# Two banded layers: transposes by halves of rows, one PSUM bank per half, and a group norm moved ahead of the inverse roots

## The chip, the core and the metric

The kernel runs on one core of a Trainium2 chip. The metric is the device time of one execution in microseconds (us); lower is better. Five engines work side by side and are ordered only by semaphores: TensorE (PE in the profile, with its weight loads shown as PEld), VectorE (DVE), ScalarE (ACT), GpSimd (POOL) and SyncE (SP), which here issues the DMAs.

## The reference

Two layers of the same form act on an image x of 512 x 512 points with 64 channels, all in float32. Cut to one layer:

```python
g = group_norm(x)                      # 32 groups of 2 channels, over the whole image
xn = ln(g)                             # over the 64 channels
left  = (xn @ Wl + bl) * mask * sigmoid(xn @ Wlg + blg)
right = (xn @ Wr + br) * mask * sigmoid(xn @ Wrg + brg)
gate  = sigmoid(xn @ Wog + bog)        # 128 hidden channels each
out[i, j] = sum over k in i-4..i+4 of left[k, i] * right[k, j]    # per hidden channel
x = x + (ln(out) * gate) @ Wo + bo
```

## The kernel before

**Tiles.** The rows are cut into blocks of 64 with an overlap of 8 (`row_blocks`, L67), and the columns into chunks of 128. Partitions 0 to 63 hold the 64 rows of the block in the left half of the columns, partitions 64 to 127 the same rows in the right half. A `Unit` (L371) is 8 columns of that: a tile z of 128 partitions x 8 columns x 64 channels. A chunk has 16 units, and there are 18 chunks a layer.

**A unit's way.** `load` (L379) brings z by DMA. `affine` (L415) applies the group norm with two tensor operations on GpSimd (z<-z,ga and z<-z,gb). `inner_stats` (L420) takes the channel statistics on VectorE (sti<-z). `inner_norm` (L424) takes the mean off and multiplies by the inverse root on GpSimd (z<-z,sti and z<-z,rs). `transposed` (L430) turns z on TensorE, four transposes of 128x128 into one PSUM bank, and ScalarE copies them to the tile zT with 1.0 added, which also goes to DRAM for later. `right` (L459) projects zT in two calls of `projected` (L447), each into a pair of banks; ScalarE makes the sigmoid sg, and VectorE multiplies (RO<-banks,sg) into RO, the buffer of 128 hidden channels for a chunk. `left` (L469) does the same for the nine diagonals of the band, at the start of a layer only.

**Mixing and the way out.** `mix` (L511) makes the banded sum for 8 channels with 16 matmuls into a pair of banks; ScalarE and VectorE copy the halves back to RO. `out_stats` (L543) takes statistics of RO (sto<-RO). `norm` (L582) writes the normalized result into the tile on (one buffer), with eight ScalarE operations. `gates` (L594) projects the gate from the recalled zT (zg) into two banks, and ScalarE makes two tiles gate. `turned` (L613) transposes on with eight transposes of 128x128 into two banks, and VectorE adds ob and multiplies by the gate into ZH. `end` (L643) projects with Wo into one bank, VectorE adds the residual XR, and SyncE stores. `biased` (L637) adds the bias to XR on GpSimd. `sums` (L662), in layer one only, adds up the second layer's group statistics into acc.

**The inverse roots.** `solve` (L549) makes, once in four steps, the inverse roots for the inner and the outer norm: VectorE prepares the variances and a first guess rs, and GpSimd refines it in ten small operations and makes two more (`rsqrt`, L134).

**PSUM.** `one_bank` (L128) takes from a pool of three single banks in layer one and four in layer two; `two_banks` (L131) takes from two pairs that projections and mixes share.

**Order.** The function `layer` (L674) writes the order out by hand: for each step t it issues the parts, and every engine keeps that order, since the helper class InOrder (L354) records each operation. So nearly all lines of the profile carry one number, L362, the helper's, and one goes by the names of the tiles. In a step t the order is: loads and recalls; statistics of RO; affine of the units planned for t; gates of t; half of the inner statistics; projections of t; inner_norm for t+2; transposed for t+1; turned and biased for t; the rest of the statistics; end of t-1; sums of t-2; the solve, where t is 3 modulo 4; norm for t+1; the mixes planned for t. Of the 16 steps of a chunk (t modulo 16), steps 0 to 9 have mixes (2, 1, 2, 2, 1, 2, 1, 2, 2, 1) and steps 10 to 15 have none. Outputs begin 30 steps after the first unit, so a layer is 30 steps of input alone, 258 of both, and 30 of output alone. The statistics of RO fall once in a step, twice in steps 10 and 11, and not at all in 8 and 9. An affine falls once in a step, twice in steps 2 and 6, and not at all in 11 and 15.

Of the kernel before, what the change touches and what calls it, by code (L numbers as in the profile page):

```python
# [8 lines left out]
F32 = mybir.dt.float32  # L9
I32 = mybir.dt.int32  # L10
AF = mybir.ActivationFunctionType
ALU = mybir.AluOpType
# [4 lines left out]
P = 128  # L17
WIN = 4
NEAR = 2 * WIN + 1
S = 64  # L20
JC = 128
JW = 16
JU = 8
JQ = 4
NU = JC // JU
# [54 lines left out]
def tile_two_banded_layers(  # L80
# [8 lines left out]
    H = layers[0]["Wl"].shape[1]  # L89
    x, out = x[0], out[0]  # L90
# [22 lines left out]
    ident = const.tile([P, P], F32, name="ident")  # L113
# [239 lines left out]
    w = views(pack)  # L353
# [70 lines left out]
    def inner_norm(u: Unit):  # L424
        z = u.z.rearrange("p (k t) c -> p k t c", t=2)
        m = u.mean.unsqueeze(3).broadcast_to([P, JU // 2, 2, D])
        en.gpsimd.tensor_tensor(z, z, m, ALU.subtract)
        en.gpsimd.tensor_tensor(u.z, u.z, last(u.rs, D), ALU.mult)

    def transposed(u: Unit):  # L430

        u.t = ztp.tile([P, JU // 2, P], F32, tag="zT", name="zT")
        pt = one_bank()
        for k in range(JU // 2):
            en.tensor.transpose(
                pt[:, k * P : (k + 1) * P],
                u.z[:, 2 * k : 2 * k + 2, :].rearrange("p j c -> p (j c)"), ident,
            )
        en.scalar.activation(u.t.rearrange("c k p -> c (k p)"), pt, AF.Identity, bias=1.0)
        if u.near is None:  # L440
            en.sync.dma_start(later[u.at], u.t)

    def place(k: int, e: int) -> int:

        return k // 2 * 4 + 2 * e + k % 2
# [136 lines left out]
    def norm(o: Out):  # L582
        o.on = onp.tile([P, JU, H], F32, tag="on", name="on")
        for j in range(JU):
# [8 lines left out]

    def gates(o: Out, w: dict):  # L594
        b = o.blk
        o.g = []
        pgs = [
            one_bank()[:, : 2 * JQ * b.m].rearrange("h (k p) -> h k p", p=b.m) for e in range(2)
        ]
# [7 lines left out]
        for pg in pgs:  # L607
            g = gp.tile([H, 2 * JQ * (S - WIN)], F32, tag="gate", name="gate")
            g = g[:, : 2 * JQ * b.m].rearrange("h (k p) -> h k p", p=b.m)
            en.scalar.activation(g, pg, AF.Sigmoid)  # L610
            o.g.append(g)

    def turned(o: Out, w: dict):  # L613

        b = o.blk
        for e in range(2):
            pt = one_bank()
            for k in range(JQ):
                en.tensor.transpose(
                    pt[:, k * P : (k + 1) * P], o.on[:, place(k, e), :], ident  # L620
                )
            zh = ZH[(2 * o.n + e) % len(ZH)]
            en.vector.scalar_tensor_tensor(
                zh[:, :, : b.m], pt.rearrange("h (k p) -> h k p", p=S)[:, :, b.lo : b.hi], w["ob"], o.g[e],
                ALU.add, ALU.mult,
            )

    def rows_of(v: bass.AP, o: Out, e: int):
# [14 lines left out]
    def end(dst: bass.AP, o: Out, w: dict):  # L643
        m = o.blk.m
        po = one_bank().rearrange("i (j c) -> i j c", c=D)
        for k in range(JQ):
            for e in range(2):
                for n in range(2):

                    en.tensor.matmul(  # L650
                        po[n * S : (n + 1) * S, 2 * k + e, :],
                        lhsT=ZH[(2 * o.n + e) % len(ZH)][:, 2 * k + n, :], rhs=w["Wo"],
                        start=True, stop=True,
                    )
# [19 lines left out]
    def layer(src: bass.AP, dst: bass.AP, w: dict, stats: bool, then=None):  # L674
# [27 lines left out]
        for n in range(0, NEAR * JQ, JU):  # L702
            t = 3 + n // JU * 2
# [3 lines left out]
        def inputs(t: int) -> list:  # L707
            return [d[t] for d in (units, lefts) if t in d]
# [3 lines left out]
        loads, affines, inners = {}, {}, {}  # L712
# [14 lines left out]
        for u in early:  # L727
            load(src, u)
        yield
        A, sti, sto = {}, {}, None  # L730
        for t in range(min(loads), last_t + 3):
            if then and t == max(units) + 2:
                then()
# [10 lines left out]
            for o in looks.get(t, []):  # L744
                if sto is None:
                    sto = sm.tile([P, NB // 2, 6], F32, tag="sto", name="sto"), []
# [1 line left out]
                for k in range(JU // 2):  # L748
                    out_stats(o, st[:, len(os) * (JU // 2) :], k)
                os.append(o)  # L750
            for u in affines.get(t, []):
                affine(u, en.vector if u.at < NU + 4 else en.gpsimd)
            if t in outs:
                gates(outs[t], w)

            todo = []
            for at, u in inners.get(t, []):
# [4 lines left out]
                n = len(us) * (JU // 2)  # L762
# [10 lines left out]
                    left(lefts[t], q, w)  # L773
            for u in inputs(t + 2):
                inner_norm(u)
            for u in inputs(t + 1):
                transposed(u)
            if t in outs:
                turned(outs[t], w)
                biased(outs[t], w, stats)  # L780
            for v in todo[len(todo) // 2 :]:
                inner_stats(*v)
# [4 lines left out]
            if t % 4 == 3:  # L787
                st, us = sti.pop((t + 5) // 4, (None, []))
                so, os = sto or (None, [])
                sto = None  # L790
                if us or os:
                    solve(w, us, os, st, so)
            if t + 1 in outs:
                norm(outs[t + 1])
            for n, (c, h0) in enumerate(mixes.get(t, [])):
                mix(c, A[c, h0 // HA], h0, [True, n + 1 < len(mixes[t])])

# [128 lines left out]
```

## Time and profile before

| | |
|---|---|
| median of 3 runs | 5162.48 us (5158.28 to 5162.59) |
| profiled execution | 5160.82 us |
| its span, first to last instruction | 5158.9 us |
| granted TensorE clock, mean | 0.970 |
| chain that ended last: share on TensorE | 73% (POOL 9%, DVE 5%, DMA 5%) |
| transposes of z | 2344 of 128x128, 395.6 us busy |
| transposes of on | 4608 of 128x128, 632.3 us busy |
| ScalarE's norm (on) | 4608, 494 ns each |
| GpSimd waited for VectorE's rs | 512.8 us in 148 waits |

A line of the profile gives source line, engine, operation, the tile written <- the tiles read, and the shapes; in the view in order of time it begins with the start from the span's beginning and the length, and in brackets stands how long the engine had been idle and who released it. "64*128" in a TensorE line is the part of the array used, rows x columns. A float32 matmul shows as two records, a transpose as one. A record of TensorE lasts longer than the distance to the next, because matmuls are pipelined: the distance between starts is what a matmul takes away from the engine.

### The profile page before, as it was taken

Reading aid. Unit: us, or ns where it says so; the run is one execution under the profiler, and the core shown is the slowest. Engines: PE = TensorE matmul, PEld = TensorE weight load, DVE = VectorE, ACT = ScalarE, POOL = GpSimd, SP = SyncE. Lnnn points to the kernel's source line nnn. Section 1 sums busy time; section 2 is a strip of 40 time slices with the busy share of each in tenths; the row PEclk is TensorE's granted clock in tenths of the full one; section 3 lists DMA queues with packets and bytes.
Section 4 is the critical chain, followed back from the end, with each engine's and each line's share of the span. In section 5 each row is a group of like instructions: output and inputs, shape, how many; then the busy total and the mean of one; then the engine's idle time right before and its main releaser. Section 6 shows DMA issues by size and latency. Waiting matters only on the chain.

```text
span 5158.9 us, 159784 instructions
## 1 busy us (share of the span) xinstructions
PE 4536.4 (88%) x60138; PEld 3756.4 (73%) x60138; DVE 3656.7 (71%) x9445; ACT 3793.4 (74%) x8328; POOL 3821.0 (74%) x4739
## 2 busy tenths in 40 slices
PE   1037999999999999999995599999999999999999
PEld 0025788888888888888873378888888887888886
DVE  6864677777777777777766467777777777777776
ACT  0013788888888888888884268888888888888888
POOL 0037888888888888888733588888888888888863
PEclk9988999999999999999998799999999999999999
DMA  7924666666666666666663457667677776667766
GB/s 318 387 62 127 176 190 191 190 192 190 193 190 190 190 191 190 191 192 192 187 169 108 105 172 200 196 197 200 194 200 199 199 199 195 194 199 200 200 186 172
DMA packets 905291, 981.45 MB, mean 190 GB/s; under 512 B 114210, under 2 KB 641608, under 8 KB 900168
## 3 DMA queue, kind: packets, MB, share of 16 engines
q1 hardware_dynamic: 897248, 948.49, 63.6%
q10 hardware_dynamic: 7272, 22.73, 1.1%
q8 instruction: 477, 7.82, 0.7%
q14 instruction: 294, 2.41, 0.2%
HBM read 658.42 MB, written 312.46 MB: 188 GB/s over the span
## 4 chain that ended last, share of the span: by engine, by line
PE 73%; POOL 9%; DMA 5%; DVE 5%; ACT 3%; issue 2%; SPq 2%; another core or an unknown queue 0%; ACTq 0%; POOLq 0%; DVEq 0%
PE banks L362 37%; PE bank L362 34%; POOL z L362 5%; POOL rsqrt L362 2%; DMA left_of<-nothing 2%; ACT on L362 2%; PE acc L362 2%; SPq L362 2%; DVE RO L362 1%; DVE ZH L362 1%; DMA gn_x<-in_x_dram 1%; POOL rs L362 1%; DMA z<-mid_x 1%; ACT gate L362 1%; DVE sti L362 0%
## 5 line engine op out<-in xcount | busy, mean ns | idle before, releaser
L362 ACT ACTIVATE on<-RO,nm,rs 128x128 f32<-128x128 f32 x4608 | 1878.3, 494 | 183.9 <-PE bank L362 178.3
L362 PE MATMUL banks<-pack,zT 64*128 64x256 f32 x9360 | 1219.7, 389 | 133.9 <-ACT zT L362 79.3
L362 PEld LDWEIGHTS banks<-pack,zT 64*128 64x128 f32 x9360 | 974.4, 193 | 413.6 <-issue 172.7
L362 PE MATMUL banks<-RO,A 64*64 64x128 f32 x18432 | 1154.6, 277 | 0.0
L362 PEld LDWEIGHTS banks<-RO,A 64*64 64x64 f32 x18432 | 1082.4, 183 | 26.7 <-issue 3.3
L362 ACT ACTIVATE sg<-banks 128x512 f32<-128x512 f32 (+1 forms) x1188 | 684.0, 589 | 323.4 <-PE banks L362 207.0
L362 DVE TENSOR_TENSOR RO<-banks,sg 128x512 f32<-128x512 f32 x1152 | 748.8, 682 | 231.0 <-ACT sg L362 230.1
L362 DVE COPY RO<-banks 128x512 f32<-128x512 f32 x360 | 249.0, 692 | 930.6 <-ACT RO L362 930.6
L362 DVE SCALAR_TENSOR_TENSOR ZH<-bank,pack,gate 128x448 f32<-128x448 f32 (+1 forms) x1152 | 742.6, 684 | 99.2 <-PE bank L362 61.4
L362 DVE BATCH_NORM_STATS2 sto<-RO 128x6 f32<-128x256 f32 x2304 | 797.8, 412 | 1.2
L362 POOL TENSOR_TENSOR z<-z,gb 128x512 f32<-128x512 f32 x536 | 685.2, 1278 | 42.0
L362 POOL TENSOR_TENSOR z<-z,ga 128x512 f32<-128x512 f32 x536 | 685.8, 1280 | 0.1
L362 PE MATMUL bank<-zg,pack 64*128 64x448 f32 (+1 forms) x2304 | 665.5, 597 | 18.6 <-DVE ZH L362 16.3
L362 PE MATMUL bank<-pack,ZH 128*64 128x64 f32 x18432 | 677.9, 228 | 3.0 <-ACT zT L362 0.5
L362 PEld LDWEIGHTS bank<-pack,ZH 128*64 128x64 f32 x18432 | 597.9, 140 | 103.6 <-ACT zT L362 76.7
L362 ACT ACTIVATE gate<-bank 128x448 f32<-128x448 f32 (+1 forms) x1152 | 566.5, 542 | 128.8 <-PE bank L362 127.9
L362 POOL TENSOR_TENSOR z<-z,rs 128x512 f32<-128x512 f32 x586 | 617.7, 1054 | 46.0
L362 PE MATMUL bank<-ident,on 128*128 128x128 f32 x4608 | 632.3, 279 | 14.7 <-ACT gate L362 12.1
L362 POOL TENSOR_TENSOR z<-z,sti 128x512 f32<-128x512 f32 x586 | 623.4, 1064 | 0.0
L362 ACT COPY RO<-banks 128x512 f32<-128x512 f32 x792 | 440.1, 585 | 225.7 <-PE banks L362 224.6
L362 DVE BATCH_NORM_STATS2 sti<-z 128x6 f32<-128x128 f32 x2344 | 549.0, 283 | 66.6 <-POOL z L362 66.6
L362 PEld LDWEIGHTS bank<-ident,on 128*128 128x128 f32 x4608 | 532.9, 144 | 73.9 <-ACT on L362 24.2
(137 smaller groups left out, 3725.3 us busy)
## 6 DMA issues: line engine op xcount, KB each, us to landing
later<-zT SPq DMA_DIRECT2D x576, 256.0 KB
A<-left_of SPq DMA_DIRECT2D x576, 256.0 KB
zg<-later SPq DMA_DIRECT2D x576, 256.0 KB
z<-in_x_dram SPq DMA_DIRECT2D x576, 128.0 KB
z<-mid_x SPq DMA_DIRECT2D x576, 128.0 KB
gn_x<-in_x_dram SPq DMA_DIRECT2D x16, 4096.0 KB
XR<-in_x_dram SPq DMA_DIRECT2D x448, 112.0 KB
mid_x<-XR SPq DMA_DIRECT2D x448, 112.0 KB
```

The costliest lines, as they stand in the source:

```text
L362: return lambda *a, **k: tc.keep_in_program_order(f(*a, **k))
```

## The change

1. **Transposes by halves.** In `transposed` and `turned` each 128x128 transpose becomes two of 64 rows: partitions 0 to 63 and 64 to 127, each with its own 64x64 corner of the identity, in the 64*128 tiling that projections and gate use. The two halves write into different PSUM banks. So there are eight transposes with 64 moving columns for z, and 16 for on.
2. **Banks.** In steady state z goes into a pair of `two_banks`; lefts and the units up to number 16 use two single banks. The copy to zT is split off into `kept`; it reads both banks in one operation, or takes two operations for the single banks. on goes into two single banks by half of the rows rather than by columns, so ZH is now filled by halves, and `end` reads it accordingly. The gate becomes one tile of twice the size, with one buffer.
3. **Order within a step.** turned comes ahead of transposed, three of the eight norm operations for t+1 come between the transposes of z and their copy, and the other five stay where norm was.
4. **Group norm ahead of the roots.** In a step with a solve (t modulo 4 is 3, beyond the first chunk) the affine operations planned for t+1 are issued on GpSimd just ahead of the solve.

```diff
@@ def transposed
+        if u.near is None and u.at > NU:
+            u.pt = [two_banks().rearrange("c (n x) -> c n x", n=2)[:, :, : JU // 2 * S]]
+            halves = [u.pt[0][:, n] for n in range(2)]
+        else:
+            halves = [one_bank()[:, : JU // 2 * S] for n in range(2)]
+            u.pt = [h.unsqueeze(1) for h in halves]
+        for k in range(JU // 2):
+            for n in range(2):
+                part = slice(n * S, (n + 1) * S)
+                en.tensor.transpose(
+                    halves[n][:, k * S : (k + 1) * S],
+                    u.z[part, 2 * k : 2 * k + 2, :].rearrange("p j c -> p (j c)"),
+                    ident[part, part],
+                )
+
+    def kept(u: Unit):
         u.t = ztp.tile([P, JU // 2, P], F32, tag="zT", name="zT")
-        pt = one_bank()
-        for k in range(JU // 2):
-            en.tensor.transpose(
-                pt[:, k * P : (k + 1) * P],
-                u.z[:, 2 * k : 2 * k + 2, :].rearrange("p j c -> p (j c)"), ident,
-            )
-        en.scalar.activation(u.t.rearrange("c k p -> c (k p)"), pt, AF.Identity, bias=1.0)
+        to = u.t.rearrange("c k (n p) -> c n k p", n=2)
+        for n, pt in enumerate(u.pt):
+            en.scalar.activation(
+                to[:, n : n + pt.shape[1]], pt.rearrange("c n (k p) -> c n k p", p=S),
+                AF.Identity, bias=1.0,
+            )
@@ def gates
-            g = gp.tile([H, 2 * JQ * (S - WIN)], F32, tag="gate", name="gate")
+        g = gp.tile([H, 4 * JQ * (S - WIN)], F32, tag="gate", name="gate")
@@ def turned
+        pts = [one_bank().rearrange("h (x p) -> h x p", p=S) for n in range(2)]
         for e in range(2):
-            pt = one_bank()
             for k in range(JQ):
-                en.tensor.transpose(
-                    pt[:, k * P : (k + 1) * P], o.on[:, place(k, e), :], ident
-                )
-            zh = ZH[(2 * o.n + e) % len(ZH)]
+                for n, pt in enumerate(pts):
+                    part = slice(n * S, (n + 1) * S)
+                    en.tensor.transpose(
+                        pt[:, e * JQ + k, :], o.on[part, place(k, e), :], ident[part, part]
+                    )
+        for n, pt in enumerate(pts):
             en.vector.scalar_tensor_tensor(
-                zh[:, :, : b.m], pt.rearrange("h (k p) -> h k p", p=S)[:, :, b.lo : b.hi], w["ob"], o.g[e],
-                ALU.add, ALU.mult,
+                ZH[(2 * o.n + n) % len(ZH)][:, :, : b.m], pt[:, :, b.lo : b.hi], w["ob"],
+                o.g[:, n], ALU.add, ALU.mult,
             )
@@ def end
-                        lhsT=ZH[(2 * o.n + e) % len(ZH)][:, 2 * k + n, :], rhs=w["Wo"],
+                        lhsT=ZH[(2 * o.n + n) % len(ZH)][:, e * JQ + k, :], rhs=w["Wo"],
@@ def layer
-            for u in affines.get(t, []):
+            for u in affines.pop(t, []):
                 affine(u, en.vector if u.at < NU + 4 else en.gpsimd)
+            if t % 4 == 3 and t > NU:
+                then_affine = affines.pop(t + 1, [])
...
+            if t in outs:
+                turned(outs[t], w)
             for u in inputs(t + 1):
                 transposed(u)
+            if t + 1 in outs:
+                norm(outs[t + 1], 0, 3)
+            for u in inputs(t + 1):
+                kept(u)
             if t in outs:
-                turned(outs[t], w)
                 biased(outs[t], w, stats)
...
+                for u in then_affine:
+                    affine(u, en.gpsimd)
+                then_affine = []
                 if us or os:
                     solve(w, us, os, st, so)
             if t + 1 in outs:
-                norm(outs[t + 1])
+                norm(outs[t + 1], 3, JU)
@@ pools
-    gp = ctx.enter_context(tc.tile_pool(name="gp", bufs=2))
+    gp = ctx.enter_context(tc.tile_pool(name="gp", bufs=1))
```

More of the change, by code (lines that the diff above doesn't have):

```diff
@@ L580, in solve, with norm @@
                 o.rs, o.nm = ro[:, n * JU : (n + 1) * JU], nm[:, n * JU : (n + 1) * JU]
-    def norm(o: Out):
-        o.on = onp.tile([P, JU, H], F32, tag="on", name="on")
-        for j in range(JU):
+    def norm(o: Out, j0: int, j1: int):
+        if j0 == 0:
+            o.on = onp.tile([P, JU, H], F32, tag="on", name="on")
+        for j in range(j0, j1):
             en.scalar.activation(
@@ L595, in gates @@
         b = o.blk
[L596 to L599, printed above, removed]
+        n = 2 * JQ * b.m
+        pgs = [one_bank()[:, :n].rearrange("h (k p) -> h k p", p=b.m) for e in range(2)]
         for e, pg in enumerate(pgs):
@@ L606, in gates @@
             )
-        for pg in pgs:
-            g = gp.tile([H, 2 * JQ * (S - WIN)], F32, tag="gate", name="gate")
-            g = g[:, : 2 * JQ * b.m].rearrange("h (k p) -> h k p", p=b.m)
-            en.scalar.activation(g, pg, AF.Sigmoid)
-            o.g.append(g)
+        g = gp.tile([H, 4 * JQ * (S - WIN)], F32, tag="gate", name="gate")
+        for e, pg in enumerate(pgs):
+            en.scalar.activation(
+                g[:, e * n : (e + 1) * n].rearrange("h (k p) -> h k p", p=b.m), pg, AF.Sigmoid
+            )
+        o.g = g[:, : 2 * n].rearrange("h (x n p) -> h n x p", n=2, p=b.m)
     def turned(o: Out, w: dict):
         b = o.blk
+        pts = [one_bank().rearrange("h (x p) -> h x p", p=S) for n in range(2)]
         for e in range(2):
-            pt = one_bank()
             for k in range(JQ):
-                en.tensor.transpose(
-                    pt[:, k * P : (k + 1) * P], o.on[:, place(k, e), :], ident
-                )
-            zh = ZH[(2 * o.n + e) % len(ZH)]
+                for n, pt in enumerate(pts):
[4 more added lines that the diff above has]
+        for n, pt in enumerate(pts):
             en.vector.scalar_tensor_tensor(
-                zh[:, :, : b.m], pt.rearrange("h (k p) -> h k p", p=S)[:, :, b.lo : b.hi], w["ob"], o.g[e],
-                ALU.add, ALU.mult,
+                ZH[(2 * o.n + n) % len(ZH)][:, :, : b.m], pt[:, :, b.lo : b.hi], w["ob"],
+                o.g[:, n], ALU.add, ALU.mult,
             )
@@ L729, in layer @@
         yield
-        A, sti, sto = {}, {}, None
+        A, sti, sto, then_affine = {}, {}, None, []
         for t in range(min(loads), last_t + 3):
```

## The prediction

> **What bounds the kernel now.** I read the page's busy shares first, then one step on TensorE and the same step on VectorE in the order of time, then GpSimd in a step without mixing, then the totals of the waits. All times are from the one profiled execution (5160.82 us); start times of single records are quoted where a merged line hides them.
>
> ```profile
> PE 4536.4 (88%) x60138; PEld 3756.4 (73%) x60138; DVE 3656.7 (71%) x9445; ACT 3793.4 (74%) x8328; POOL 3821.0 (74%) x4739
> ```
>
> TensorE at 88% is 96% inside the layers (96.55 of 100 us in the stretch from 1500 to 1600). One step with one mix, TensorE, columns start, length, what:
>
> ```profile
> 1506.58 1.02 PE L362 MATMUL bank<-zg,pack 64*128 64x448 f32 x4
> 1507.44 1.89 PE L362 MATMUL banks<-pack,zT 64*128 64x256 f32 x16
> 1509.26 0.66 PE L362 MATMUL bank<-ident,z 128*128 128x128 f32 x4
> 1509.76 1.04 PE L362 MATMUL bank<-ident,on 128*128 128x128 f32 x8
> 1510.72 1.15 PE L362 MATMUL bank<-pack,ZH 128*64 128x64 f32 x32
> 1511.70 0.64 PE L362 MATMUL acc<-XR 120*64 120x65 f32 x16
> 1512.27 2.10 PE L362 MATMUL banks<-RO,A 64*64 64x128 f32 x32
> ```
>
> No line starts with a wait: this step is TensorE's work alone, 7.72 us to the next gate. I count from its gate: second projection issued by 2.58, transposes from 2.68 to 4.05, mix from 5.69. VectorE in the same step:
>
> ```profile
> 1507.32 0.69 DVE L362 COPY RO<-banks 128x512 f32<-128x512 f32 x1 [3.81 <-ACT RO L362]
> 1507.93 1.40 DVE L362 BATCH_NORM_STATS2 sto<-RO 128x6 f32<-128x256 f32 x4
> 1509.24 0.48 DVE L362 BATCH_NORM_STATS2 sti<-z 128x6 f32<-128x128 f32 x2
> 1509.63 1.28 DVE L362 TENSOR_TENSOR RO<-banks,sg 128x512 f32<-128x512 f32 x2
> ```
>
> This chain hangs on the end of the previous mix: copy, eight statistics, then the product of `right`. The first product ends at 1509.63+0.68 = 1510.31, 3.72 after the gate. Nobody needs it before the mix at 5.69 today: 1.9 us of slack. GpSimd, six steps later, and TensorE's answer:
>
> ```profile
> 1548.68 1.19 POOL L362 TENSOR_TENSOR XR<-XR,fewer 120x512 f32<-120x512 f32 x1 [2.04 <-PE bank L362]
> 1556.16 0.29 POOL L362 TENSOR_TENSOR rsqrt<-rs 128x64 f32<-128x64 f32 x1 [6.29 <-DVE rs L362]
> ```
>
> ```profile
> 1560.68 1.27 POOL L362 TENSOR_TENSOR z<-z,ga 128x512 f32<-128x512 f32 x1
> 1562.03 1.27 POOL L362 TENSOR_TENSOR z<-z,gb 128x512 f32<-128x512 f32 x1
> 1563.26 1.06 POOL L362 TENSOR_TENSOR z<-z,sti 128x512 f32<-128x512 f32 x1
> 1564.39 1.04 POOL L362 TENSOR_TENSOR z<-z,rs 128x512 f32<-128x512 f32 x1
> ```
>
> ```profile
> 1565.49 0.66 PE L362 MATMUL bank<-ident,z 128*128 128x128 f32 x4 [2.55 <-POOL z L362]
> ```
>
> GpSimd sits 6.29 us idle for VectorE's `rs`, then does the roots, then the group norm, and only then the z that TensorE waits for.
>
> **What the skill says.** "TensorEngine Tiling (Array Packing)", Key Properties: a change of tiling mode drains TensorE, and tiles work in parallel. The trace agrees: the eight projection pairs issue every 0.216 (the two of a pair 7 ns apart), so the next could start at 1509.17, but z starts at 1509.26 and its first transpose takes 0.165 instead of 0.109. A change costs 0.09 + 0.06 = 0.15 us. The same page, Gotcha 1, wants different row tiles in different PSUM banks, which is why each half gets a bank. "TensorE: Matmul & The Clock Gate", PE-mode transpose, gives about 275 ns for a bf16 transpose in a kernel; here the record lasts 279 to 293, but the next starts after 109, and 109 is what I use. "PSUM — Partial Sum Buffer", Engine vs sequencer instructions: VectorE, ScalarE and GpSimd are strict FIFO; the lines above show it, the group norm does not pass the waiting roots.
>
> **Part 1, transposes by halves.** Per step 12 transposes (4 of z, 8 of on) become 12 pairs with 64 moving columns each. No row shows a transpose in 64*128 tiles. Nearest: `bank<-pack,ZH`, 64 columns in pairs, 16 pairs from 1510.72 to 1511.70, less 0.05 for the first = 0.058 a pair. The weight side allows that: the second LDWEIGHTS of the 128x128 transposes starts 58 ns after the first. I take 0.058. Bounds: 0.054 (half of 109), and 0.116, if the halves of a pair follow each other or if the weights take as long as the gate's 64x128 ones (its first pair lasts 0.107 longer than its second). TensorE saves 12×(0.109−0.058) = 0.61, and the mode change behind the projection (0.15): 0.76 us a step, if nothing else comes in.
>
> **Part 2, where the halves go.** In the order of the changed program, z goes into `two_banks`, two buffers that projections and mixes share; its first transpose waits for a VectorE count that is the first product of `right`, and for GpSimd's z. Behind it on TensorE stand the output projection, the sums and the mix. So in a step behind a mix: on ends at 2.58+8×0.058 = 3.05; z starts at 3.72+0.055 (the hand-over from VectorE, as from ZH at 1547.48 to 1547.54) = 3.77, 0.72 stalled; it takes 0.056 for its first weights and 4×0.058, to 4.06; from the transposes' end to the mix is 1.64 as before: 5.70. Before: 5.69. **The saving is spent on a wait.** The steps of a chunk, by t mod 16: 1, 2, 4, 5, 6 have this product at 3.72: +0.01 each. In 3 and 7 two units' statistics put it at 4.12: +0.41 each. In 8 and 9 no statistics of RO stand ahead, 3.31: −0.40 each. Step 0: −0.08. Sum over the ten mixing steps: about 0. The later zT copy (behind three `on`) ends near 5.1, ahead of the second mix that needs its bank at 7.5: free. ScalarE's eight `on` end at 7.15, before the mix does: free.
>
> **Part 3, steps 10 to 15, without mix.** Steps 10 to 12 are VectorE's (6.2 of 6.4 us busy, eight RO statistics each in the first two). z stalls there up to 2.2 us, but TensorE's later results still arrive before VectorE's queue comes to them, so VectorE keeps its pace: layer one 18.85 instead of 19.05, layer two 18.5 instead of 18.1. At the solve of step 11 the group norm for step 12 (2×1.29 = 2.58) now runs inside the 6.29 idle; its z was loaded at 1540.7. So the z for step 13 is ready 2.58 sooner, and the 8.31, 9.88 or (layer two) 10.5 us of step 13 fall to ScalarE's pace: gates 0.88, sg 1.04, zT 0.52, on 8×0.394 = 3.15, 5.6 us, its 0.34 wait for the transposes being gone since on is transposed first and three `on` lie ahead of zT. Steps 14 and 15 go at the same 5.6; GpSimd needs 5.87 with a group norm in each, but starts 2.58 ahead: its z is ready 0.3 to 0.6 before it is wanted. Layer one: 18.85+3×5.62 = 35.7, against 39.1 and 40.4 in alternate chunks (1541.14 to 1580.24, 1668.60 to 1709.00): −4.05. Layer two: 35.2 against 39.06 (4235.44 to 4274.50): −3.9. With 15 such chunks a layer: 61+58 = 119 us. The other solves gain nothing; TensorE does not wait there.
>
> **Part 4, the ends.** Each layer's first 30 steps: z shorter by 0.2 in ten mixing steps (4 us for both layers), and the 5.31 and 4.12 us waits for POOL at 541.56 and 3031.16 shorter by 2.58 (5). Ten mixing steps per layer after the last unit have no z and no stall: 8×0.051+0.15 = 0.56 each (11). Twenty last steps of layer one go at 4.50 because `on` and its transposes alternate on one buffer; the transposes shrink by 0.45 there (9). Together 29. The gate tile (one buffer for two halves) costs nothing: ScalarE's gate comes after both ZH products today as well.
>
> **Sum.** 5160.8−119−29 = 5013 for the profiled execution; it lies 1.7 below the median of the runs shown, so 5014.
>
> **Rivals.** (a) Pairs at 0.116: z ends at 4.29, +0.23 in 310 mixing steps (71) and some 10 at the ends: 5095. The gate's weights speak for it, the transposes' 58 ns against. (b) No cost of the z wait, if VectorE's product comes sooner than I read: ten steps gain 0.6 to 0.76, 310×0.7 = 215 more: about 4800. TensorE's 96% speaks for it, the 3.72 against. (c) Slower: a half-transpose costs as much as a whole one and halves do not overlap, 0.218 a pair. on ends at 4.32, z at 5.25, +1.19 in 310 mixing steps, 370 us lost, and some 60 in steps 13 to 15, against 148 gained: about 5440. It decides from about 0.16 a pair (z must end by 4.06+0.48). The profile has no transpose in this tiling, so it can't be excluded; the projections' pairs, 7 ns apart, speak against it.
>
> **Chances.** Forecast 0.73, (a) 0.11, (b) 0.05, (c) and other losses 0.11. Unsure in the forecast itself: ScalarE's pace in steps 13 to 15 (at 5.9 instead of 5.6: +27), the hand-over (0.1 instead of 0.055: +14), pairs at 0.054 and a shorter chain (−30). With (a)'s end inside, 4975 to 5105; (b) and (c) are left out. Faster by over 0.2% (what a measurement of this kernel can tell from no change): 0.87; within: 0.03; slower: 0.10.
>
> **What would show it.** Single starts of the new transposes 58 ns apart per pair; TensorE idle ahead of `banks<-ident,z`, released by DVE RO, of 300 to 400 us in all (0.7 in most mixing steps, about 2 in step 10); steps 1 to 9 of a chunk unchanged in sum at 79 us in layer one, steps 13 to 15 at about 5.6 each; GpSimd's 512.8 us of waiting for `rs` (the waits' total) down by 150 to 200, half of it in step 11. I am wrong if the pairs lie further apart than 60 ns, if mixing steps shorten by over 0.2 on average, or if step 13 stays above 7.

## The result, and the profile after

| | before | after |
|---|---|---|
| median of the runs | 5161.35 us (5158.28 to 5162.59) | 5192.92 us (5190.45 to 5194.06) |
| ratio, 95% interval | | 1.0061 (1.0044 to 1.0079) |
| span of the profiled execution | 5158.9 us | 5191.7 us |
| granted TensorE clock, mean | 0.970 | 0.962 |

The change makes the kernel 0.6% slower; the forecast was 5014. The page's first part, for the kernel after:

```profile
PE 4206.4 (81%) x67090; PEld 3583.6 (69%) x67090; DVE 3720.7 (72%) x9445; ACT 3759.0 (72%) x8372; POOL 3825.2 (74%) x4739
```

TensorE works 330 us less than before (4536.4) and the span is 33 us longer: the transposes did get cheaper, and some 360 us of new idle time took the place of that. Where it lies can be seen when the steps of a chunk are laid beside each other. A step is the time from one gate (`bank<-zg,pack`) to the next; means over the 15 chunks of each layer that have all 16 steps:

| steps (t mod 16) | layer one, before | after | layer two, before | after | both layers, 15 chunks each |
|---|---|---|---|---|---|
| 0 | 9.63 | 12.40 | 9.48 | 13.08 | +96 us |
| 1 to 9, sum | 78.75 | 79.75 | 74.53 | 75.47 | +29 us |
| 10 to 12, sum | 19.06 | 19.65 | 18.10 | 18.82 | +20 us |
| 13 to 15, sum | 20.74 | 16.86 | 21.06 | 16.43 | -128 us |

With what lies around these chunks (+16 us) that makes the 33 us of the spans. Step 13 lost its stall, as forecast; **one step in sixteen, step 0, takes three quarters of that back** (96 of 128 us). One such step before, VectorE and then TensorE, in the order of time (start, length, what; in brackets how long idle before and released by whom):

```profile
1580.98 0.67 DVE L362 TENSOR_SCALAR var<-sti 128x32 f32<-128x32 f32 x1
...
1582.01 0.20 DVE L362 TENSOR_SCALAR rs<-var 128x64 int32<-128x64 int32 x1
```

```profile
1582.92 0.66 PE L362 MATMUL bank<-ident,z 128*128 128x128 f32 x4
...
1585.99 3.95 PE L362 MATMUL banks<-RO,A 64*64 64x128 f32 x64
```

TensorE in one such step after:

```profile
1717.41 1.02 PE L362 MATMUL bank<-zg,pack 64*128 64x448 f32 x4
...
1720.00 0.66 PE L362 MATMUL bank<-ident,on 64*128 64x64 f32 x16
1722.95 0.46 PE L362 MATMUL banks<-ident,z 64*128 64x64 f32 x8 [2.30 <-POOL rsqrt L362]
...
1724.33 1.09 PE L362 MATMUL acc<-XR 120*64 120x65 f32 x16
1725.35 4.96 PE L362 MATMUL banks<-RO,A 64*64 64x128 f32 x64
```

The transposes of z stand 2.30 us idle. The named releaser, GpSimd's `rsqrt`, is only the count that came last by the profile; what z needs is its pair of banks, and that is VectorE's first product of `right`. After the stall the same instructions take longer: the sums 1.09 where other steps have 0.64, the two mixes 4.96 instead of 3.94. VectorE, from the third of the solve's five operations on, and GpSimd:

```profile
1718.58 1.05 DVE L362 TENSOR_SCALAR var<-var 128x32 f32<-128x32 f32 x1
1719.54 0.17 DVE L362 TENSOR_SCALAR nm<-sto 128x32 f32<-128x32 f32 x1
1719.66 1.24 DVE L362 TENSOR_SCALAR rs<-var 128x64 int32<-128x64 int32 x1
1720.82 1.39 DVE L362 BATCH_NORM_STATS2 sto<-RO 128x6 f32<-128x256 f32 x4
1722.14 1.27 DVE L362 TENSOR_TENSOR RO<-banks,sg 128x512 f32<-128x512 f32 x2
```

```profile
1718.29 1.30 POOL L362 TENSOR_TENSOR XR<-XR,fewer 120x512 f32<-120x512 f32 x1
1719.55 1.30 POOL L362 TENSOR_TENSOR z<-z,ga 128x512 f32<-128x512 f32 x1
```

Two of the solve's small VectorE operations, `var<-var` on 32 columns and `rs<-var` on 64, last 1.05 and 1.24 us. The first starts 0.29 after GpSimd's `XR<-XR` does and ends at 1719.63, as that operation ends (1719.59); the second starts 0.11 after the moved group norm's first operation and ends at 1720.90, as that one does (1720.85). VectorE's statistics and the product come behind them in its order: the first product ends 5.4 us after the gate.

The Trainium skill has this in "SBUF — State Buffer", Who interferes with whom: VectorE and GpSimd share a pair of ports as a lock, an operation of VectorE in a 2-port mode (tensor_scalar can be one) or with two inputs in SBUF contends for it, and whoever comes second blocks for the other's whole instruction. The trace agrees, and shows which operations are spared. Medians (of the lengths) over all records of the kernel after, without and with a GpSimd operation beside them:

| VectorE operation | alone | beside GpSimd | records beside |
|---|---|---|---|
| rs<-var | 0.195 us | 1.233 us | 40 |
| var<-var | 0.181 us | 1.051 us | 32 |
| var<-sti | 0.170 us | 0.676 us | 46 |
| sti<-z (statistics) | 0.280 us | 0.281 us | 1876 |
| sto<-RO (statistics) | 0.409 us | 0.409 us | 2100 |
| RO<-banks,sg (reads PSUM) | 0.680 us | 0.681 us | 934 |
| var<-sto (two inputs in SBUF) | 0.188 us | 0.186 us | 36 |
| nm<-sto | 0.175 us | 0.169 us | 32 |
| z<-z,gb on VectorE, 128x512 (two inputs in SBUF) | 0.691 us | 1.411 us | 30 |

The last row comes from the start of the layers; the 16 of its 30 records that begin beside GpSimd's 128x512 `z<-z,rs` take 1.41 us, the others 0.69. So it is not only small operations that are held. `var<-sto` and `nm<-sto` are mostly spared in this kernel; in `nm<-sto` above, VectorE starts just as one GpSimd operation gives way to the next. In e2_group_norm_only below both are stretched too. Of the solve's five operations 97 records in the kernel after last over 0.4 us: each begins while a GpSimd operation runs and ends within 0.06 us of the end of one. The profile before already held 25 such records; the `var<-sti` of 0.67 us above is one, beside GpSimd's `XR<-XR`.

The span of the solve's five operations ahead of step 0 is 0.94 and 0.75 us before (layers one and two, means of 16 chunks) and 2.84 and 3.21 after; ahead of the other solves it stays at 0.72 to 0.85 after. Before, GpSimd mostly sat waiting for `rs` while VectorE made it. The change filled just that waiting time with the group norm.

The last part of the loss is TensorE's clock. The same stretch cut into windows (columns: window, length, busy time of PE, PEld, DVE, ACT, POOL with instructions, then the granted clock, the busy share of the DMA engines and GB/s):

```profile
1720.00:1723.00 3.00, 0.70 (x20) 0.59 (x17) 3.00 (x7) 2.06 (x5) 2.76 (x5) 1.00 0.71 208
1723.00:1724.30 1.30, 1.30 (x40) 1.23 (x42) 1.30 (x3) 0.85 (x2) 1.05 (x4) 1.00 0.79 267
1724.30:1727.71 3.41, 3.41 (x46) 3.29 (x42) 0.98 (x2) 1.68 (x5) 2.92 (x8) 0.50 0.77 223
1727.72:1731.00 3.28, 3.28 (x50) 2.89 (x48) 0.01 (x1) 1.66 (x3) 3.20 (x4) 1.00 0.24 76
```

Full clock until 1.35 us after the end of the stall, then half the clock for 3.41 us, then full again. What decides this is looked at under "The clock" below.

### The profile page after: what moved, and what is told of

Same layout as the page of the kernel before. It is cut to its first block, busy times and chain, and to the rows that moved or that the text cites. A ratio compares the mean times of both kernels' runs of the same rounds, so it can differ in the third digit from the quotient of the medians.

```text
span 5191.7 us, 173015 instructions
## 1 busy us (share of the span) xinstructions
PE 4206.4 (81%) x67090; PEld 3583.6 (69%) x67090; DVE 3720.7 (72%) x9445; ACT 3759.0 (72%) x8372; POOL 3825.2 (74%) x4739
## 5 line engine op out<-in xcount | busy, mean ns | idle before, releaser
L362 ACT ACTIVATE on<-RO,nm,rs 128x128 f32<-128x128 f32 x4608 | 1934.1, 498 | 12.3 <-PE bank L362 12.1
L362 PE MATMUL banks<-pack,zT 64*128 64x256 f32 x9360 | 1176.9, 391 | 104.3 <-ACT zT L362 54.5
L362 PEld LDWEIGHTS banks<-pack,zT 64*128 64x128 f32 x9360 | 939.5, 195 | 412.5 <-issue 195.4
L362 PE MATMUL banks<-RO,A 64*64 64x128 f32 x18432 | 1175.3, 280 | 14.3 <-ACT zT L362 14.3
L362 PEld LDWEIGHTS banks<-RO,A 64*64 64x64 f32 x18432 | 1103.4, 184 | 41.4 <-ACT zT L362 17.1
L362 PE MATMUL bank<-zg,pack 64*128 64x448 f32 (+1 forms) x2304 | 617.8, 606 | 2.5 <-DVE ZH L362 2.4
L362 PE MATMUL banks<-ident,z 64*128 64x64 f32 x4336 | 254.8, 234 | 443.0 <-DVE RO L362 267.6
L362 POOL TENSOR_TENSOR XR<-XR,pack 120x512 f32<-120x512 f32 (+1 forms) x352 | 418.7, 1190 | 198.2 <-DMA XR<-mid_x 87.7
```

Source lines behind the costliest of these rows:

```text
L362: return lambda *a, **k: tc.keep_in_program_order(f(*a, **k))
```

## Experiments

Three theories. **T:** in step 0 GpSimd's work blocks VectorE's solve; the product comes late; z waits for it because of its new bank; TensorE idles and gets a lower clock. **R1:** GpSimd is merely late, since the group norm stands ahead of the roots. **R2:** z's new bank alone makes step 0 slow, and the group norm is harmless. "Five" is the mean span of the solve's five VectorE operations ahead of step 0, layers one and two.

| kernel | median us | ratio to before (95%) | step 0, layers one, two | five |
|---|---|---|---|---|
| e1_group_norm_back | 5211.6 | 1.0093 (1.0077 to 1.0110) | 10.00, 11.11 | 1.52, 1.99 |
| e2_group_norm_only | 5070.4 | 0.9823 (0.9808 to 0.9838) | 9.93, 9.87 | 3.10, 2.71 |
| e3_not_at_15 | 5131.3 | 0.9939 (0.9924 to 0.9954) | 10.13, 11.03 | 1.57, 2.16 |
| e7_behind_first_root | 5131.7 | 0.9937 (0.9922 to 0.9952) | 10.14, 11.46 | 1.58, 2.12 |
| e8_bias_too | 5099.6 | 0.9878 (0.9863 to 0.9893) | 9.65, 9.70 | 0.72, 1.38 |
| e4_z_behind_sums | 4981.6 | 0.9650 (0.9636 to 0.9664) | 9.78, 11.61 | 2.61, 3.26 |
| e9_both | 4937.2 | 0.9564 (0.9549 to 0.9580) | 9.01, 8.76 | 0.72, 1.43 |
| e10_on_by_halves | 5216.2 | 1.0105 (1.0090 to 1.0120) | 10.25, 8.90 | 0.72, 1.95 |
| e12_group_norm_no_collision | 5073.1 | 0.9824 (0.9811 to 0.9838) | 9.67, 9.17 | 0.72, 0.72 |
| e13_all_but_11 | 4918.1 | 0.9528 (0.9515 to 0.9541) | 9.01, 8.76 | 0.72, 1.37 |

### The change without the group norm, and the group norm without the change

```diff
@@ layer, against the kernel after (e1_group_norm_back)
-            if t % 4 == 3 and t > NU:
-                then_affine = affines.pop(t + 1, [])
...
-                for u in then_affine:
-                    affine(u, en.gpsimd)
-                then_affine = []
```

> The changed kernel with the group norm back in its old place (part 4 undone); transposes by halves, banks and order as changed. Theory T: in step 0 of a chunk the moved group norm runs on GpSimd while VectorE does the five small operations of the solve; they share something, VectorE's are held for whole GpSimd operations (span of the five 3.17 us instead of 0.72), the first product of `right` comes 1.6 us late, z waits for it, TensorE idles 2.3 us and is then granted a lower clock. So without the moved group norm step 0 goes back from about 12.9 to 9.7 us (31 steps, -98), while step 13 gets its stall back (+2.6 in 30 chunks and the two ends, +82): about 5177 us, the five operations back at 0.72. Rival R2, the bank of z alone makes step 0 slow and the group norm is harmless: step 0 stays at 12.9, about 5275. Rival R1, GpSimd is merely late: 5177 as T.

Measured 5211.6, slower than the kernel after. Step 13 has about half of its stall back (7.68 and 7.73 us, where it took 9.12 and 10.36 before), and step 0 falls to 10.00 and 11.11, against R2. But it does not reach 9.7, and the five take 1.5 to 2.0 us, not 0.72: I had missed that other work of GpSimd runs into the solve by itself in the changed order, the bias on XR in both layers and the inner norm's `z<-z,rs`, mostly in layer two.

```diff
@@ layer, against the kernel before (e2_group_norm_only)
-            for u in affines.get(t, []):
+            for u in affines.pop(t, []):
                 affine(u, en.vector if u.at < NU + 4 else en.gpsimd)
+            if t % 4 == 3 and t > NU:
+                then_affine = affines.pop(t + 1, [])
...
+                for u in then_affine:
+                    affine(u, en.gpsimd)
+                then_affine = []
                 if us or os:
                     solve(w, us, os, st, so)
```

> The kernel before with part 4 alone: the group norm ahead of the solve, whole transposes in their old banks and order. T: the five operations of VectorE's solve take 3.2 us here too, but z waits for no product and the mix only from 5.69 after the gate, so step 0 stays at 9.6; step 13 loses its stall: 5161-82 = 5079 us. R2: the same time, but the five operations at 0.72. R1, a late GpSimd is what delays step 0: step 0 near 12.6, about 5175 us.

Measured 5070.4 against T's 5079. The collision is there in full, and it costs 0.3 and 0.4 us a step (9.63 and 9.48 before). VectorE and then TensorE in one step 0 of this kernel:

```profile
1683.50 1.32 DVE L362 SCALAR_TENSOR_TENSOR var<-sto,pack 128x32 f32<-128x32 f32 x1
...
1684.95 1.27 DVE L362 TENSOR_SCALAR nm<-sto 128x32 f32<-128x32 f32 x1
```

```profile
1684.86 0.66 PE L362 MATMUL bank<-ident,z 128*128 128x128 f32 x4
...
1688.28 3.94 PE L362 MATMUL banks<-RO,A 64*64 64x128 f32 x64 [0.28 <-DVE RO L362]
```

Others of the five are stretched here than in the kernel after: whichever happens to meet a GpSimd operation. That speaks for a shared resource and against a semaphore of one of them. z has its own bank and waits for nothing; only the mix waits, 0.28 us, for the second product. So the collision alone is nearly free, and R1 (5175) is out for this kernel.

### The group norm at step 15: early, late, or beside nothing

```diff
@@ layer, against the kernel after (e3_not_at_15)
-            if t % 4 == 3 and t > NU:
+            if t % 4 == 3 and t > NU and t % NU != NU - 1:
```

> The changed kernel, with the group norm ahead of the solve in steps 3, 7 and 11 of a chunk but at its old place for step 0. T: step 0 falls from 12.9 to 9.7 us with TensorE at full clock, steps 1 to 15 stay: 5193-98 = 5095 us. R1: the same. R2: step 0 stays at 12.9, 5193 us.

```diff
@@ rsqrt, solve, layer, against the kernel after (e7_behind_first_root)
         e.tensor_tensor(t, o, o, ALU.mult)
+        if then:
+            then()
         e.tensor_tensor(t, t, v, ALU.mult)
...
-                for u in then_affine:
-                    affine(u, en.gpsimd)
+                def late(us=then_affine):
+                    for u in us:
+                        affine(u, en.gpsimd)
...
+                if t % NU != NU - 1:
+                    late()
                 if us or os:
-                    solve(w, us, os, st, so)
+                    solve(w, us, os, st, so, late if t % NU == NU - 1 else None)
...
```

> The changed kernel, but in the solve of step 15 the group norm is issued on GpSimd just behind the first small operation of the roots, which waits for VectorE's rs: GpSimd has the same work before its roots are done and is as late as in the changed kernel, but can no longer run beside VectorE's five operations. T: the five at 0.72 us, step 0 at 9.7, 5193-98 = 5095 us. R1, GpSimd is merely late (the roots and what follows them): step 0 stays near 12.9, 5193 us. R2: 5193 us.

5131.3 and 5131.7: both 61 us below the kernel after, where T had said 98. In the second, GpSimd does the same work before its roots are done and is just as late: its roots end 9.4 and 10.2 us after the gate of step 0, in the kernel after 9.2 and 10.0, in e3_not_at_15 only 6.9 and 7.8. The group norm merely starts behind an operation that needs VectorE's finished `rs`. The same time for both puts R1 out as the cause of this loss (it gave 5193), and R2 with it. The missing 37 us showed in the five operations, 1.6 and 2.1 us: the bias on XR again, and in layer two `z<-z,rs` with it. The next kernel sends the bias behind the first root as well:

```diff
@@ layer, against the last kernel (e8_bias_too)
-            if t in outs:
+            if t in outs and (t % NU != NU - 1 or not (sto or sti.get((t + 5) // 4))):
                 biased(outs[t], w, stats)
...
-                def late(us=then_affine):
+                def late(us=then_affine, o=outs.get(t)):
+                    if o and t % NU == NU - 1:
+                        biased(o, w, stats)
...
```

> The last kernel of the first four (group norm of step 15 behind the first operation of the roots), with the bias on XR of that step put behind that operation as well, so that no GpSimd operation at all can run beside VectorE's solve in step 0. There the five operations still took 1.7 us instead of 0.72, because this bias ran beside one of them, and step 0 took 10.0 (layer one) and 11.4 us (layer two). T: 0.72 us, step 0 at 9.7 and 9.6: 5132-(0.35*16+1.8*15) = about 5100 us. Rival, what is left in step 0 comes from GpSimd's lag or the clock: no change, 5132 us.

Measured 5099.6. The same step 0 as above, VectorE and TensorE:

```profile
1693.93 0.20 DVE L364 TENSOR_SCALAR rs<-var 128x64 int32<-128x64 int32 x1
1694.04 1.40 DVE L364 BATCH_NORM_STATS2 sto<-RO 128x6 f32<-128x256 f32 x4
1695.45 1.52 DVE L364 TENSOR_TENSOR RO<-banks,sg 128x512 f32<-128x512 f32 x2
```

```profile
1696.29 0.46 PE L364 MATMUL banks<-ident,z 64*128 64x64 f32 x8 [0.24 <-DVE RO L364]
...
1698.23 3.94 PE L364 MATMUL banks<-RO,A 64*64 64x128 f32 x64
```

`rs<-var` is short again (so are the other four), z waits 0.24 instead of 2.30, the mixes are back at 3.94. (In layer two `var<-sti` still meets `z<-z,rs` in 14 of 15 steps, hence the 1.38 of the table.) Two small reorderings on GpSimd take 93 us off the kernel after (5192.9 to 5099.6), which is the size of step 0's loss (96 us). So the collision with VectorE's solve is the cause of that loss.

### The wait of z

```diff
@@ layer, against the kernel after (e4_z_behind_sums)
+        def to_z(t: int):
+            for u in inputs(t + 1):
+                transposed(u)
+            if t + 1 in outs:
+                norm(outs[t + 1], 0, 3)
+            for u in inputs(t + 1):
+                kept(u)
...
-            for u in inputs(t + 1):
-                transposed(u)
-            if t + 1 in outs:
-                norm(outs[t + 1], 0, 3)
-            for u in inputs(t + 1):
-                kept(u)
+            if t not in mixes:
+                to_z(t)
...
                 sums(outs[t - 2], t - 2 == first_t, t - 2 == last_t)
+            if t in mixes:
+                to_z(t)
```

> The changed kernel; in steps with a mix TensorE's transposes of z (with the three norms and the copy that hang on them) come behind the output projection and the sums instead of ahead of them. Theory T: z's wait for the first product of `right` is what eats the saving of the transposes. With 1.6 us of other work ahead of z the wait is covered in steps 1 to 9 (0.6 us less each, 279 steps, -167) and in step 0 too, where the mix then waits only for the second product (5.4 us after the gate): 9.8 instead of 12.6, 31 steps, -87. About 4940 us, steps 1 to 9 of layer one at 73.2 us in sum. Rival: the wait only replaces other limits (another bank or the copy zT is late next), so little is gained in steps 1 to 9 and only step 0 comes back: about 5105. Rival: a denser TensorE is granted a lower clock (0.96 to 0.93): about 5060 with the waits gone.

Measured 4981.6: 211 us less than the kernel after from a change of order alone (of z's transposes, the three norms and the copy). Steps with one mix fall from 7.85 to 7.15 us in layer one; steps 2 and 5 with two mixes by only 0.4 (9.68 to 9.23 and 9.69 to 9.27), since their second projection now lies 0.26 later. Steps 1 to 9 sum to 74.3, not 73.2. Layer two's step 0 still takes 11.61: the product comes 6.1 us after the gate there, later than the output projection covers. The rival of a lower clock through denser work (5060) did not come.

The two edits together (e9_both: this one and that of e8_bias_too):

> Both edits together: z behind the sums, and nothing of GpSimd beside the solve of step 0. T: z waits for no product any more, so the collision costs only what the second product makes the mix late (about 0.3 us in 31 steps): about 4930 us, 10 below the kernel with z behind the sums alone. Rival, VectorE's lost time counts by itself in step 0: 4880 us or less, 50 below it.

Measured 4937.2, 44 below the kernel with z behind the sums, where I had said 10 and the rival 50; the rival was nearer. Step 0 gives 54 us of it (9.78 to 9.01 and 11.61 to 8.76, 15 chunks each), and steps 4 and 8 give some back. So the collision still cost much under the cover. I had taken its delay from one step of layer one; it is longer in layer two (without this edit the first product ends 6.14 us after the gate there, 5.25 in layer one).

```diff
@@ layer, against e9_both (e13_all_but_11; the same in three more places)
-                if t % NU != NU - 1:
+                if t % NU not in (3, 7, 15):
                     late()
```

> The kernel of both edits (4937 us: z behind the sums, nothing of GpSimd beside the solve of step 0), with the same done for the solves of steps 3 and 7 as well: group norm and bias behind the first operation of the roots, except at step 11, whose group norm must stay ahead. In the kernel of both edits the solves before steps 4 and 8 still took 2.8 us (both layers) and 1.3 and 3.0 us; steps 4 lay 0.36 and 0.38 above the same kernel with z behind the sums alone, and step 8 of layer two 0.73. T: these come back in 15 chunks, -22: about 4915 us. Rival, those collisions are hidden and the excess has another cause: 4937 us.

Measured 4918.1, by T. A step with two mixes on TensorE in this kernel (compare the first one of the prediction, which has one mix):

```profile
1656.99 0.67 PE L364 MATMUL bank<-ident,on 64*128 64x64 f32 x16
...
1658.56 0.64 PE L364 MATMUL acc<-XR 120*64 120x65 f32 x16
1659.13 0.46 PE L364 MATMUL banks<-ident,z 64*128 64x64 f32 x8
1659.52 3.94 PE L364 MATMUL banks<-RO,A 64*64 64x128 f32 x64
```

Nothing stalls behind the projections (these take 2.15 instead of 1.89), and the mix starts 5.37 us after the gate. This version beats both kernels, by 4.7% and 5.3%.

### Two that missed

Only `on` by halves, z whole in one single bank of its own:

```diff
@@ transposed, layer, against e3_not_at_15 (e10_on_by_halves)
+            for u in inputs(t + 1):
+                u.pt = one_bank()
             if t in outs:
                 turned(outs[t], w)
...
         for k in range(JU // 2):
-            for n in range(2):
-                part = slice(n * S, (n + 1) * S)
-                en.tensor.transpose(
-                    halves[n][:, k * S : (k + 1) * S],
-                    u.z[part, 2 * k : 2 * k + 2, :].rearrange("p j c -> p (j c)"),
-                    ident[part, part],
-                )
+            en.tensor.transpose(
+                u.pt[:, k * P : (k + 1) * P],
+                u.z[:, 2 * k : 2 * k + 2, :].rearrange("p j c -> p (j c)"), ident,
+            )
```

> The kernel with the group norm not moved at step 15, and z again in whole 128x128 transposes in one single bank of its own; only `on` is transposed by halves (order on, z). T: z waits for no product, so the 8 pairs of `on` save 8*0.05 = 0.4 us in each mixing step against the kernel before (7.31 and 9.15 us in layer one, 73.9 in sum for steps 1 to 9); with steps 10 to 15 as in the changed kernel: 5131 - 310*0.47 - about 20 in step 0 = about 4965 us. Rival, the halves save nothing by themselves on TensorE: steps 1 to 9 at 77.7 as before, about 5075 us.

Measured 5216.2. Layer two, with four single banks, did what was expected: most steps 6.88 and 8.71 us instead of 7.26 and 9.09, 0.38 less. Layer one has three, and its steps rose by 0.82 (8.55, 10.39), for a wait that the totals of the waits name (us in all, times, longest):

```profile
PEld bank L362 <- DVE ZH L362: 446.5, 389, 2.8
```

(Before, this wait was 58.9 us.) With two banks for the halves of `on` and one for z, the output projection gets a bank that VectorE's ZH must empty first. So of the two arrangements that were run, z in `two_banks` is the cheaper one for layer one; the bank has its price either way.

The group norm alone, with GpSimd kept off the solve of step 15 (against e2_group_norm_only the edits of e7_behind_first_root and e8_bias_too):

> The kernel before (whole transposes in their old banks and order) with part 4 alone, and at step 15 the group norm and the bias on XR behind the first operation of the roots, so that nothing of GpSimd runs beside VectorE's solve in step 0. T: against the kernel with part 4 alone (5070 us), whose step 0 took 9.9 us in both layers, step 0 goes back to 9.63 and 9.48 as before, 31*0.35: about 5060 us. The five operations back from 3 us to 0.72. So a collision of the same length costs 0.35 us here and 3.2 in the changed kernel, since here only the mix waits for VectorE's products, and for the second of them. Rival, step 0's 0.35 is GpSimd's lateness: 5070 us.

Measured 5073.1, no gain over 5070.4, though step 0 went back (9.67 and 9.17). Layer two's step 1 rose from 7.26 to 7.91; one of them on TensorE:

```profile
3122.64 0.66 PE L364 MATMUL bank<-ident,z 128*128 128x128 f32 x4 [0.56 <-POOL z L364]
```

GpSimd's z comes late now that step 0 is shorter. Here R1's mechanism is real: where a collision costs 0.3 us, what is put behind the roots to avoid it costs as much.

### The clock

Ten experiments and the two kernels give 360 steps 0 in whole chunks. In 53 the two mixes take over 3.8 us from first to last start (3.67 at full clock), and all 53 had TensorE idle for at least 1.6 us ahead of them in that step; of the 280 steps with shorter idle times none was slowed. 27 steps had an idle time as long and were not slowed. So the idle time is needed and not enough.

The traces show what else decides. The granted clock has only two values in them, 1.00 and 0.50, and changes only on a grid of 3.41 us that is fixed within an execution. Of the grid's windows at full clock between the first gate of layer one and the last of layer two (15,198 in the twelve traces), 368 were followed by a window at half clock. The estimate "half clock follows where TensorE's records cover less than 47% of a window" (each window read 0.1 us early) finds 336 of them and is wrong in 48 windows in all; the 47% and the 0.1 us are fitted to these same traces. In the steps above it holds for 49 of the 53 slowed ones and for 24 of the 27 others: an idle time of 2 us within one window costs clock, the same one spread over two windows mostly does not. No run changed the clock alone, so this is a rule of these traces and not a tested cause.

Against e8_bias_too, step 0 of the kernel after is 2.8 and 3.4 us longer; 1.0 and 1.5 us of that lie behind the start of z's transposes, where the slow records are. The mean clock of a whole execution, as in the tables, says little: the kernel before showed 0.970 and 0.946 in two executions of 5161.0 and 5161.3 us.

## Why the prediction was wrong

**The step that failed** is the end of Part 3: "The other solves gain nothing; TensorE does not wait there." It costed the moved group norm at nothing in step 15, and Part 2 gave "Step 0: −0.08". Nothing is gained there indeed, but the move also puts GpSimd's operations beside VectorE's solve, and these block. The prediction took the time that GpSimd waits for `rs` as free to fill. I looked at what stands behind the group norm on GpSimd, and not at who shares GpSimd's ports. The runs put +2.8 and +3.6 us in place of -0.08, 96 us in 30 steps. The parts of the miss, 5193 against 5014 (by the spans of the two profiled executions, +33 instead of -148 us):

| term | predicted | measured | miss, us |
|---|---|---|---|
| step 0, 30 chunks | -2 | +96 | 98 |
| steps 1 to 9 | +2 | +29 | 27 |
| steps 10 to 15 | -119 | -108 | 11 |
| around these chunks | -29 | +16 | 45 |

**Part 1** was right but for a small size: new transposes lie 0.062 us apart by pairs instead of 0.058, just over the 60 ns that the prediction had named as a sign of being wrong. The mode change is gone, and TensorE's busy time fell by 330 us. Layer two of e10_on_by_halves shows the saving by itself, 0.38 a step where eight pairs should give 0.41.

**Part 2** had the mechanism right and one size off. After a mix, VectorE's first product ends 3.73 us after the gate (3.72 predicted) and z starts at 3.87: the hand-over takes 0.14, not the 0.055 taken from ZH. The step in the kernel after:

```profile
1741.98 0.46 PE L362 MATMUL banks<-ident,z 64*128 64x64 f32 x8 [0.62 <-DVE RO L362]
...
1743.92 3.94 PE L362 MATMUL banks<-RO,A 64*64 64x128 f32 x64
```

The mix starts at 5.81 instead of 5.70. So steps 1, 2, 4, 5 and 6 lose 0.12 instead of 0.01, steps 3 and 7 lose 0.47 and 0.51 in layer one (0.41 predicted), 8 and 9 gain 0.29 (0.40 predicted). The waits' total for this line looks as forecast (300 to 400):

```profile
PE banks L362 <- DVE RO L362: 309.4, 384, 9.7
```

Not all of it is z's: the line holds 42 us of the projections as well. z's transposes waited 268 us for DVE RO, and 79 us more, most of it in step 0, stand under `rsqrt`. That this wait eats the saving is shown by e4_z_behind_sums, which moves it behind other work and gains 0.7 us in the steps with one mix.

**Part 3** held for steps 13 to 15: 16.86 in layer one, three times the predicted 5.62, and 16.43 in layer two (16.7). Steps 10 to 12 were to take 18.85 and 18.5, and took 19.65 and 18.82. Step 10's wait of z is the predicted 2 us; after it TensorE's records are long as in step 0:

```profile
1815.30 0.46 PE L362 MATMUL banks<-ident,z 64*128 64x64 f32 x8 [2.07 <-DVE RO L362]
...
1817.86 1.87 PE L362 MATMUL bank<-zg,pack 64*128 64x448 f32 x4
```

The gate takes 1.87 instead of 1.02; I had given VectorE the pace of these steps. GpSimd's waiting for `rs` fell by 47 us only (512.8 to 466.0, predicted 150 to 200): by 2.4 (layer one) and 2.0 us ahead of step 12, near the 2.58 of the forecast, and by 1.2 us ahead of step 0, while ahead of steps 4 and 8 it rose by 0.2 to 1.0, which I did not follow up.

**Part 4** was wrong in sign. In the ten mixing steps per layer without z, layer one went from 5.90 and 7.73 us to 6.00 and 7.83, where I had -0.56; layer two gained 0.31. In layer one a pair of halves needs both of its banks at once, and the second is free only when ScalarE has read the first half of the gate: in one such step the first of the 16 transposes of `on` starts 0.91 us after the gate, the other 15 wait for ScalarE's gate, with TensorE idle for 0.65 us, and run from 1.78 to 2.49. Before, four of the eight transposes ran ahead of that release. In the last twenty steps, 4.50 before and 4.56 after, the transposes wait for the same release. The transposes did not set these steps' pace; I had taken their busy time for it. These steps are the smaller part of the +16 us: 8 us lie in the sixteenth chunk of each layer, where step 0 comes once more, and 10 us in the stretches ahead of each layer's first gate (5.2 and 4.5), which stay unexplained.

Of the **rivals** none was this. (a) and (c) were about the pairs' price, and (b) took the wait of z, which did come, for absent. My rival on the slow side had the wrong mechanism; the right one takes two of the change's edits together. By these runs the group norm alone is -92 us (e2_group_norm_only), the rest of the change +49 (e1_group_norm_back), the two together +32: 75 us come from their meeting.

## What to carry to other kernels

A neighbour's waiting time is free only if what fills it shares nothing with the one it waits for. When work is moved on GpSimd, list the VectorE operations that will run beside it, look which of them are tensor operations from SBUF to SBUF (statistics were spared here), and ask who waits for what is queued behind them. GpSimd's operations that started only behind the solve's last result did not collide with it; that cost nothing where they had slack, and as much as the collision where they had none. And a cheaper instruction gives its time back when its new bank hangs on a later release: cover that wait with other work (here the output projection and the sums) before counting the saving.

## What was not expected of the hardware

- VectorE operations of 0.17 to 0.20 us lasted up to 1.05 to 1.32 us beside a GpSimd tensor operation, and ended with it, while statistics of SBUF and products with a PSUM operand did not change by 1% beside it.
- A float32 transpose by halves in 64*128 tiles runs as a pair in 0.062 us, where the whole one takes 0.109.
- The granted TensorE clock was halved for 3.41 us (6.83 in five cases) in 53 of 80 steps 0 with idle times of 1.6 us and more; whether it was, went mostly by how much of one window of a fixed grid of 3.41 us TensorE's records covered, with about 47% as the limit in these traces.
